# Four moves in an eight-stage layer stack: batch 0's preparation among feed-forward steps, keys beside the search for places, later results behind a lead, split maxima with priority

## The chip, the cores and the metric

The kernel runs on one core of a Trainium2 chip. A core has five engines with instruction queues of their own, each worked off in order: TensorE (PE in the profile; its weight loads are PEld), VectorE (DVE), ScalarE (ACT), GpSimd (POOL) and SyncE (SP), which here issues most DMA transfers. Engines wait for each other through semaphores. The metric is the device time of one execution in microseconds (us). Before the change the median of 3 runs is 3196.8 us (3187.31 to 3198.38).

## The reference

The input `x` has 4 batches of 512 rows of 512 numbers; a context `ctx_1024` has 4 x 512 rows of 256. Four layers each add a mixing block and a feed-forward block to `x`, each on the layer norm of `x` and behind a gate:

```python
x = x + tanh(g_xattn[0]) * L0_xattn(_layernorm(x), ctx_1024, ...)   # stage 0
x = x + tanh(g_ffn[0])   * L0_ffn(_layernorm(x), ...)               # stage 1
x = x + tanh(g_xattn[1]) * L1_xattn(_layernorm(x), ctx_1024, ...)   # stage 2
x = x + tanh(g_ffn[1])   * L1_ffn(_layernorm(x), ...)               # stage 3
x = x + tanh(g_xattn[2]) * L2_xattn(ctx_1024, _layernorm(x), ...)   # stage 4
x = x + tanh(g_ffn[2])   * L2_ffn(_layernorm(x), ...)               # stage 5
x = x + tanh(g_xattn[3]) * L3_xattn(_layernorm(x), ctx_1024, ...)   # stage 6
x = x + tanh(g_ffn[3])   * L3_ffn(_layernorm(x), ...)               # stage 7
```

The blocks that the change touches compute this:

```python
# L0_xattn: 16 heads of 32; softmax(q k^T) v over 496 keys, and over 16 more, added
# L0_ffn: relu((x @ sign(up).T) * up_scale) @ sign(down).T * down_scale * output_scale
# L2_xattn: a state-space scan over the context, gated by the normed x as z
xc = causal_conv(in_proj_w @ ctx, conv_w, 4 taps); u = silu(xc + conv_b)
dt_lo, Bm, Cm = split(x_proj_w @ u, (16, 16, 16))
delta = softplus(dt_proj_w @ dt_lo + dt_proj_b); A = -exp(A_log)
state = state * exp(delta * A) + (delta * u) * Bm;  y_t = sum_n state * Cm
y = (y + D * u) * silu(z)
# L2_ffn: top 2 of 8 experts per row, weights normalised; expert: (silu(x Wg) * (x Wu)) Wd
# L3_xattn: 32 heads of 16, q from x, k and v from ctx, axial rope on q and k, softmax, Wout
```

The scan of L2_xattn and the keys and values of L3_xattn depend on the context alone, not on `x`.

## The kernel before

`tile_blocks_kernel` (L2056) opens pools for a group of stages, runs them and closes the pools, so that the next group's tiles take the same memory. A scheduler puts each engine's instructions in order from their recorded priority and estimated readiness; `tc.high_priority(offset=...)` shifts the priority of what is recorded inside it, and `tied=True` products keep their recorded order on PE.

Stage 0 (`s0`): for each batch and each group of four heads a turn of products makes logits `s_ps`, and DVE takes their negated maxima per row (`s_nmx`, L694). `parted` (L644) splits each maximum on GpSimd into three 16-bit parts by copies and subtractions, PE transposes these (`s_ptm`), and they come off the logits `s_pl` before the exponential. `sums` (L751) takes the sums of the exponentials (`s_ri`, with a GpSimd multiply at L765).

Stage 1 (`s1`, L868): 4 batches x 2 halves x 8 double steps, 64 steps `f2`. A step makes `s_ph` (PE, L244), `s_hT` (ACT) and, one step behind, adds to four `s_acc` (PE, L905). Twice in a step `aside(1)` takes one yield from the generator `states()` (L1047), the state-space scan of stage 4, recorded at an offset of -4000. `states()` first loads its weights and yields; then it runs the nine pieces of batch 0 (`channels` 0 to 3, `low`, `raw`, `delta`, `raw`, `delta`) in one go and yields; both of these yields are taken ahead of the steps, by `next(states)` in the main function and in `s1`. Each of the 128 further yields makes two of 256 states: `s_db` on DVE, `s_da` on ACT, the scan `s_h` on DVE (L1158), its product with `s_C` on GpSimd (L1159), and sums over states on PE (`s_y`, L268). The next batch's pieces come between them. In a piece, `channels` has a product `s_pi`, its copy `s_xp` on ACT (L1095), and four taps on DVE (`s_xc`, the first at L1097, three more at L1099); `delta` has an add of 1 on DVE (L1129 is the step after it). `channels_done` ends a group of channels with two DVE steps on `s_ru` (L1195 and L1198). The signs of the feed-forward weights are ACT passes over `s1_wu` and `s1_wd` ahead of the steps.

Stages 2 to 4 run as generators, a batch apart, in 38 turns. Every second turn takes one piece of `keys()` (L1610), stage 6's keys and values: a product `s_pkv` on PE, `rope` on DVE (six steps, L1580 to L1582), the copy `s_vs` on ACT (L1673), DMA stores to `s_vd` and `s_kd`, and, for the piece before, eight transposes `pt_s6k` with an ACT scaling `s_kt` (L1690). There are 16 pieces and a last transposition, done by the end of stage 4.

Stage 5 (`s5`, L1510): `top2` routes rows to 8 experts (`s_pr`), `places` (L1313) finds where each row goes among 39 blocks of 128 rows of one expert each (a chain of small DVE steps with products `s_before`, `s_inside`, `s_inv` on PE), then `blocks` (L1454) runs the blocks: GpSimd gathers rows `s_xb`, PE transposes them and makes `pg_s`, DVE and ACT make `g_s`, PE makes `s_po`, GpSimd scatters the result to `s_ys`. A block's weights are four loads by SP into one of `ep` = 4 buffers (L1532 to L1537), each at the address of a register that SP reads from `ofi`.

Stage 6 (`s6`, L1693): `pieces(b)` prepares a batch. `results` (L1764) loads `s_y` (two buffers), adds stage 5's results to `x` (`residual`, L863: two DVE steps per tile of rows), loads the keys `s_kT` and values `s_v`, and makes the norm's statistics (`newton`, L186). Then come `xT`, `query` with `rope`, and `queryT`. A lead of 12 slots of maxima alone (`maxima`, DVE `s_top`, L1837) precedes the slots in which the products of weights and values run beside them. The pieces of batches 1 to 3 are dealt out over the slots of the batch before.

Of the kernel before, what the change touches and what calls it, by code (L numbers as in the profile page):

```python
# [48 lines left out]
class Net:  # L49
# [228 lines left out]
    def s0(self):  # L278
# [362 lines left out]
        def maxima():  # L641
# [26 lines left out]
            for b in range(NB):  # L668
                kT, qT = made[b][0:2]
                for g in range(4):  # L670
# [31 lines left out]
                    parted(b, g, nmx)  # L702
# [165 lines left out]
    def s1(self, states, aside):  # L868
# [26 lines left out]
        next(states)  # L895
# [23 lines left out]
        for i in range(2 * NB):  # L919
            b, cols = i // 2, slice(i % 2 * HT * P, (i % 2 + 1) * HT * P)  # L920
            for f2 in range(FC // 2):
                if i % 2 and f2 == 0 and b + 1 < NB:
                    xTs[b + 1] = self.lnT(f"s1_{b + 1}", b + 1)
                ph = self.mm(f"s1_ph_{i}_{f2}").rearrange("p (j n) -> p j n", j=2)
                for j in range(2):
                    fs = slice((2 * f2 + j) * P, (2 * f2 + j + 1) * P)
                    self.chain(
                        ph[:, j, :], [(wu[c][:, fs], xTs[b][:, c, cols]) for c in range(DC)],
                        tied=True,
                    )  # L930
                aside(1)
                behind.end()
                hT = self.t(f"s1_hT_{i}_{f2}").rearrange("p (j n) -> p j n", j=2)
                for j in range(2):
                    f = 2 * f2 + j
                    nc.scalar.activation(  # L936
                        hT[:, j, :], ph[:, j, :], AF.Relu, scale=us[:, f : f + 1]
                    )
                behind(down, i, f2, hT, more=True)
                aside(1)  # L940
# [106 lines left out]
    def states(self):  # L1047
# [31 lines left out]
        def pieces(b):  # L1079
# [3 lines left out]
            def channels(e):  # L1083
# [13 lines left out]
                nc.vector.tensor_scalar(xc, xp[:, 0:S], cw[:, e, 0:1], None, op0=ALU.mult)  # L1097
# [23 lines left out]
            def delta(es):  # L1121
# [5 lines left out]
                for z, z1 in zip(zs, z1s):  # L1127
                    nc.scalar.activation(z, z, AF.Exp, scale=-1.0)
                    nc.vector.tensor_scalar(z1, z, 1.0, None, op0=ALU.add)  # L1129
                    nc.vector.scalar_tensor_tensor(z, z1, -1.0, z, op0=ALU.add, op1=ALU.subtract)  # L1130
# [48 lines left out]
        yield  # L1179
# [7 lines left out]
        def channels_done(b, e, u, y):  # L1187
# [4 lines left out]
            nc.scalar.copy(r0, y[:, 0, :])  # L1192

            def rest():
                nc.vector.scalar_tensor_tensor(  # L1195
                    u, u, vec[:, 2, e : e + 1], r0, op0=ALU.mult, op1=ALU.add
                )
                nc.vector.tensor_tensor(u, u, r, op=ALU.add)  # L1198
                nc.sync.dma_start(rows[b]["y"][e * P : (e + 1) * P, :], u)
# [298 lines left out]
    def combine(self, name, weights, tiles, out=None):  # L1498

        ys = self.sorted[name][2][0 : 2 * NT * P, :].rearrange("(i t p) n -> t p i n", i=2, p=P)  # L1500
        for t in tiles:
            y = self.bp.tile([P, 2, D], F32, tag="y2", name=f"{name}_y2_{t}", bufs=self.y2)
            self.nc.sync.dma_start(y, ys[t])
            for i, w in enumerate(weights):
                self.residual(t, y[:, i, :], w[:, t : t + 1])
# [4 lines left out]
    def s5(self):  # L1510
# [11 lines left out]
        places, ofi = self.places("s5", hots, E)  # L1522

# [169 lines left out]
    def s6(self):  # L1693
# [12 lines left out]
        made, stats = {}, {}  # L1706
# [24 lines left out]
        def pieces(b):  # L1731
# [32 lines left out]
            def results():  # L1764

                self.combine("s5", self.wt5, range(b * TB, (b + 1) * TB))
# [24 lines left out]
        def maxima():  # L1791
# [18 lines left out]
            for b in range(NB):  # L1810
                kT, qT = made[b][0:2]
                for g in range(8):
                    for t in range(TB):
                        for y in range(2):
# [19 lines left out]
                            def after(ps=ps, dst=top[g % 2][:, t, 2 * y : 2 * y + 2, 16:17]):  # L1834
                                for i in range(2):
# [4 lines left out]
                                    ps[i][1](ins)  # L1840

# [214 lines left out]
def kernel(ctx: ExitStack, tc: tile.TileContext, a: dict, out: bass.AP):  # L2056
# [18 lines left out]
    with net.pools(cp=2, kp=1, rp=1, wp=8, bp=2, tp=14, sp=2, ps2=2, ps1=4):  # L2075
# [6 lines left out]


        stages = [net.s2(), net.s3(), net.s4()]
        turns = 0
        for step in range(NB + len(stages) - 1):
            going = [f(step - i) for i, f in enumerate(stages) if 0 <= step - i < NB]
            while going:
                going = [g for g in going if next(g, going) is None]
                turns += 1  # L2090
                if turns % 2:
                    aside(1)
        for _ in keys:
            pass
    net.y2 = 2
    with net.pools(op=1, ep=4, bp=1, up=3, tp=8, sp=2, ps2=2, ps1=4):
        net.s5()
# [88 lines left out]
```

## Time and profile before

| what | us |
|---|---|
| median of 3 runs | 3196.8 |
| the profiled execution, its own time | 3203.01 |
| its span | 3201.1 |
| stage 0, start to last `s_po` | 0 to 647 |
| first and last scan of the states | 695.5 and 1427.4 |
| stages 2 to 4, from the first `s_pq` to the end of stage 4's last transposes on PE | 1448 to 1738.5 |
| routing products `s_pr`, end | 1780.4 |
| first `pg_s` of stage 5 | 1815.4 |
| a block of stage 5 | 8.335 |
| stage 6, first `s_pq` | 2170.4 |

The mean granted clock of TensorE is 0.931 of full speed. The numbers behind an engine in a row of the profile are its busy time and, behind an x, its instructions. In an answer on waits a line has the waiting engine and what it wanted to do, then the engine and operation that released it, then the total in us, how often, and the longest. Rows of groups have line, engine, operation, output and input, shape and count, then busy us and mean ns of one, then the idle time of the engine just before them and who ended it.

### The profile page before, as it was taken

The numbers are of one execution on the slowest core, as the hardware profiler recorded it, in microseconds if no ns is written. First come the engines' busy times: TensorE is split into PE (matmuls) and PEld (weight loads), VectorE is DVE, ScalarE is ACT, GpSimd is POOL, SyncE is SP. The second block draws the span as 40 slices with busy tenths as digits, with TensorE's granted clock in tenths as the row PEclk, the third lists the DMA queues.
The fourth block names the chain that finished last, engine by engine and source line by source line (L and its number), as shares of the span: only waits on it lengthen the run. The fifth ranks groups of instructions, "written<-read, shape, count | busy, mean of one in ns | idle before, by whom it ended". The sixth has DMA issues, their size and how long they took to land.

```text
span 3201.1 us, 43082 instructions
## 1 busy us (share of the span) xinstructions
PE 2821.5 (88%) x15776; PEld 1442.0 (45%) x15776; DVE 1952.0 (61%) x3212; ACT 1196.0 (37%) x2061; POOL 975.8 (30%) x939
## 2 busy tenths in 40 slices
PE   6899898768988989997786699977999999989999
PEld 2333333234444444443344588862333333345774
DVE  6565666378897979987788311118666666735004
ACT  2343443365554445433222111112554545521331
POOL 3465654516555655760000122210000000001440
PEclk8899999879999989999897699997999999989999
DMA  4000000177676767862212599973000000013996
GB/s 133 7 1 7 1 1 1 20 252 238 195 229 176 236 206 224 250 196 84 77 64 90 176 320 326 322 259 137 14 29 14 29 1 1 1 53 122 379 384 225
DMA packets 266897, 438.75 MB, mean 137 GB/s; under 512 B 32400, under 2 KB 114576, under 8 KB 265152
## 3 DMA queue, kind: packets, MB, share of 16 engines
q1 hardware_dynamic: 250624, 386.72, 37.8%
q0 software_dynamic: 13760, 45.10, 3.9%
q10 hardware_dynamic: 2304, 4.20, 0.3%
q8 instruction: 126, 2.06, 0.3%
q14 instruction: 83, 0.68, 0.1%
HBM read 370.79 MB, written 65.13 MB: 136 GB/s over the span
## 4 chain that ended last, share of the span: by engine, by line
PE 60%; DVE 16%; POOL 9%; ACT 6%; issue 6%; DMA 3%; SPq 0%; DVEq 0%; POOLq 0%; ACTq 0%
PE s_pl L268 12%; PE s_po L244 11%; PE pg_s L244 7%; PE s_ph L244 6%; POOL s_h L1159 6%; PE s_pq L244 4%; PE s_av L268 3%; ACT pr_s L1957 2%; PE s_pb L244 2%; DVE s_h L1158 2%; PE s_acc L905 2%; PE s_pkv L244 1%; PE pt_s L223 1%; DVE x L863 1%; POOL es_s L746 1%
## 5 line engine op out<-in xcount | busy, mean ns | idle before, releaser
L1159 POOL TENSOR_TENSOR s_h<-s_h,s_C 128x512 f32<-128x512 f32 x256 | 448.1, 1751 | 290.3 <-DVE s_h L1158 248.6
L268 PE MATMUL s_pl<-s_qT,s_kT 32*128 32x512 f32 (+1 forms) x1536 | 447.3, 658 | 60.4 <-ACT pr_s L846 23.5
L268 PE MATMUL s_ps<-s_kT,s_qT 32*128 32x512 f32 (+1 forms) x1536 | 441.1, 677 | 12.7 <-DVE s_top L1837 5.9
L1837 DVE TENSOR_REDUCE s_top<-s_ps 128x1 f32<-128x512 f32 x512 | 328.5, 685 | 108.7 <-PE s_ps L268 108.6
L1957 ACT ACTIVATE pr_s<-s_pl 128x512 f32<-128x512 f32 x512 | 277.9, 595 | 307.4 <-PE s_ps L268 297.7
L1158 DVE TENSOR_TENSOR_SCAN s_h<-s_da,s_db 128x512 f32<-128x512 f32 x256 | 312.1, 1219 | 62.5 <-PE s_y L268 36.1
L1157 ACT ACTIVATE s_da<-s_rdl,s_A 128x512 f32<-128x512 f32 x256 | 184.4, 722 | 329.2 <-DVE s_h L1158 328.4
L1331 POOL MEMSET s_room<- 128x128 f32 (+1 forms) x2 | 0.5, 258 | 998.9 <-PE s_av L268 678.8
L268 PE MATMUL s_av<-pr_s,s_v 128*32 128x256 f32 (+1 forms) x3072 | 250.9, 398 | 0.2
L244 PE MATMUL s_ph<-xT_s,s_wu 128*128 128x256 f32 x1024 | 247.9, 397 | 0.7 <-ACT xT_s L161 0.7
L905 PE MATMUL s_acc<-s_wd,s_hT 128*128 128x512 f32 x512 | 239.9, 612 | 5.7 <-ACT s_hT L936 5.7
L244 PEld LDWEIGHTS s_ph<-xT_s,s_wu 128*128 128x128 f32 x1024 | 198.2, 198 | 78.8 <-issue 50.2
L244 PEld LDWEIGHTS pg_s<-s_xbT,s_w 128*128 128x128 f32 (+1 forms) x1872 | 214.7, 184 | 19.8 <-issue 17.8
L268 PEld LDWEIGHTS s_pl<-s_qT,s_kT 32*128 32x128 f32 (+1 forms) x1536 | 118.4, 186 | 227.1 <-ACT pr_s L1957 95.8
L244 PE MATMUL pg_s<-s_xbT,s_w 128*128 128x128 f32 (+1 forms) x1872 | 216.2, 276 | 1.4 <-ACT s_xbT L161 1.4
L694 DVE TENSOR_REDUCE s_nmx<-s_ps 128x1 f32<-128x496 f32 x256 | 158.4, 662 | 91.6 <-PE s_ps L268 81.3
L1156 DVE TENSOR_TENSOR s_db<-s_B,s_rdu 128x512 f32<-128x512 f32 x256 | 203.8, 796 | 10.7 <-DMA s_B<-s_bc 2.8
L846 ACT ACTIVATE pr_s<-s_pl 128x512 f32<-128x512 f32 (+1 forms) x256 | 138.7, 593 | 158.9 <-PE s_pl L268 82.9
L268 PE MATMUL s_y<-s_h,ident 64*64 64x512 f32 x1024 | 147.6, 640 | 49.5 <-issue 32.3
L268 PEld LDWEIGHTS s_av<-pr_s,s_v 128*32 128x32 f32 (+1 forms) x3072 | 61.4, 109 | 286.0 <-issue 253.9
L1552 DVE TENSOR_TENSOR g_s<-g_s,pg_s 128x256 f32<-128x256 f32 x78 | 27.5, 352 | 264.5 <-ACT g_s L1551 264.5
L1446 POOL DMA_INDIRECT s_xb<-s_xs,s_from x86 | 83.2, 968 | 333.0 <-PE ptr_s_xb L234 176.1
(388 smaller groups left out, 4460.4 us busy)
## 6 DMA issues: line engine op xcount, KB each, us to landing
s_B<-s_bc SPq DMA_DIRECT2D x256, 256.0 KB
s_C<-s_bc SPq DMA_DIRECT2D x256, 256.0 KB
s_w<-in_s_wg SPq DMA_DIRECT2D x39, 704.0 KB
s_w<-in_s_wu SPq DMA_DIRECT2D x39, 704.0 KB
s_w_rt<-in_s_ru SPq DMA_DIRECT2D x47, 512.0 KB
s_w_rt<-in_s_rd SPq DMA_DIRECT2D x47, 512.0 KB
s_w<-in_s_wd SPq DMA_DIRECT2D x39, 512.0 KB
s_y<-s_ys SPq DMA_DIRECT2D x32, 512.0 KB
```

Of the source, the lines that this page charges most:

```text
L244: ins = self.nc.tensor.matmul(out, lhsT=l, rhs=r, start=(i == 0), stop=(i == len(pairs) - 1)).ins
L268: ins = self.nc.tensor.matmul(out, lhsT=l, rhs=r, **flags).ins
L694: ins = nc.vector.tensor_reduce(nmx[:, at + i : at + i + 1], ps[i][0][:, 0:M], axis=AX.X, op=ALU.max, negate=True,).ins
L846: ins = nc.scalar.activation(prs[i][0:n, j, :], pl[j][0][0:n, :], AF.Exp).ins
L905: ins = nc.tensor.matmul(accs[i][t], lhsT=hT[:, j, t * P : (t + 1) * P], rhs=wd[f // 4][:, f % 4, :], start=(f == 0), stop=(f == FC - 1),).ins
L1156: nc.vector.tensor_tensor(db, br, du, op=ALU.mult)
L1157: nc.scalar.activation(da, dl, AF.Exp, scale=am[:, e, n : n + 1])
L1158: nc.vector.tensor_tensor_scan(h, da, db, 0.0, op0=ALU.mult, op1=ALU.add)
L1159: nc.gpsimd.tensor_tensor(h, h, cr, op=ALU.mult)
L1446: self.nc.gpsimd.indirect_dma_start(out=t, out_offset=None, in_=self.sorted[name][1], in_offset=bass.IndirectOffsetOnAxis(ap=fr[:, j : j + ...
L1837: ins = nc.vector.tensor_reduce(dst[:, i], ps[i][0], axis=AX.X, op=ALU.max, negate=True).ins
L1957: ins = nc.scalar.activation(prs[i][:, j, :], pl[j][0], AF.Exp).ins
```

## The change

The edits, by stage:

- `parted` in stage 0 is recorded at high priority.
- `next(states)` in `s1` goes. `states()` yields after each of batch 0's nine pieces and then three times more, so that these run in the first calls of `aside`; the first call in a step takes two yields where the step's number is 2 modulo 5, which makes 141 calls of 128.
- In the pieces the first tap of `s_xc` and the add of 1 go from DVE to ACT. In `channels_done` the two parts of the sum are added on GpSimd, and DVE has one step of two left.
- Stages 2 to 4 take a piece of `keys()` in every fourth turn. The rest is taken in stage 5 by one call behind `places`. The pools of `keys()` stay open through stage 5, and stage 5 has three buffers of weights (`ep`) where it had four.
- In stage 6 `lead` collects the instructions of the maxima. `combine` gets the last one recorded for batches 1 to 3, and orders its residuals behind it on DVE without a semaphore.

```diff
--- before.py
+++ after.py
@@ -699,7 +699,8 @@
 
                             yield parts, olds, after
                     waiting = b, g
-                    parted(b, g, nmx)
+                    with self.tc.high_priority():
+                        parted(b, g, nmx)
             turn(*waiting)
 
         queue, now = {}, [0]
@@ -892,7 +893,6 @@
 
         behind = Behind()
         xTs = {0: self.lnT("s1_0", 0)}
-        next(states)
         accs = {}
         HT = TB // 2
 
@@ -928,7 +928,8 @@
                         ph[:, j, :], [(wu[c][:, fs], xTs[b][:, c, cols]) for c in range(DC)],
                         tied=True,
                     )
-                aside(1)
+
+                aside(2 if (i * FC // 2 + f2) % 5 == 2 else 1)
                 behind.end()
                 hT = self.t(f"s1_hT_{i}_{f2}").rearrange("p (j n) -> p j n", j=2)
                 for j in range(2):
@@ -1094,7 +1095,7 @@
                 nc.gpsimd.memset(xp[:, 0:3], 0.0)
                 nc.scalar.copy(xp[:, 3 : S + 3], pi)
                 xc = self.t(f"s4_xc_{b}_{e}")
-                nc.vector.tensor_scalar(xc, xp[:, 0:S], cw[:, e, 0:1], None, op0=ALU.mult)
+                nc.scalar.mul(xc, xp[:, 0:S], cw[:, e, 0:1])
                 for k in range(1, 4):
                     nc.vector.scalar_tensor_tensor(
                         xc, xp[:, k : S + k], cw[:, e, k : k + 1], xc, op0=ALU.mult, op1=ALU.add
@@ -1126,7 +1127,7 @@
                 z1s = [self.t(f"s4_z1_{b}_{e}") for e in es]
                 for z, z1 in zip(zs, z1s):
                     nc.scalar.activation(z, z, AF.Exp, scale=-1.0)
-                    nc.vector.tensor_scalar(z1, z, 1.0, None, op0=ALU.add)
+                    nc.scalar.add(z1, z, 1.0)
                     nc.vector.scalar_tensor_tensor(z, z1, -1.0, z, op0=ALU.add, op1=ALU.subtract)
                 for z1 in z1s:
                     nc.scalar.activation(z1, z1, AF.Ln)
@@ -1176,7 +1177,11 @@
         yield
         for piece in pieces(0):
             piece()
-        yield
+            yield
+
+        for _ in range(3):
+            yield
+
         def row(k, b, e):
             t = self.qp.tile(
                 [P, S], F32, tag=f"r{k}", name=f"s4_r{k}_{b}_{e}", bufs=1 + (k != "u")
@@ -1190,12 +1195,12 @@
             nc.scalar.copy(r[0:64], y[64:128, 1, :])
             nc.scalar.copy(r[64:128], y[0:64, 1, :])
             nc.scalar.copy(r0, y[:, 0, :])
+            nc.gpsimd.tensor_tensor(r, r, r0, op=ALU.add)
 
             def rest():
                 nc.vector.scalar_tensor_tensor(
-                    u, u, vec[:, 2, e : e + 1], r0, op0=ALU.mult, op1=ALU.add
-                )
-                nc.vector.tensor_tensor(u, u, r, op=ALU.add)
+                    u, u, vec[:, 2, e : e + 1], r, op0=ALU.mult, op1=ALU.add
+                )
                 nc.sync.dma_start(rows[b]["y"][e * P : (e + 1) * P, :], u)
 
             return rest
@@ -1495,19 +1500,27 @@
 
         return self.nc.sync.value_load(ofi[0:1, j : j + 1], min_val=0, max_val=E - 1)
 
-    def combine(self, name, weights, tiles, out=None):
+    def combine(self, name, weights, tiles, out=None, after=None):
 
         ys = self.sorted[name][2][0 : 2 * NT * P, :].rearrange("(i t p) n -> t p i n", i=2, p=P)
         for t in tiles:
             y = self.bp.tile([P, 2, D], F32, tag="y2", name=f"{name}_y2_{t}", bufs=self.y2)
             self.nc.sync.dma_start(y, ys[t])
             for i, w in enumerate(weights):
-                self.residual(t, y[:, i, :], w[:, t : t + 1])
+                ins = self.residual(t, y[:, i, :], w[:, t : t + 1]).ins
+                if after is not None:
+                    self.tc.add_manual_dep(
+                        ins, after.name,
+                        mybir.DependencyInfo(
+                            mybir.DependencyClass.NoSync, mybir.DependencyReason.DATA
+                        ),
+                        reason="order on VectorE",
+                    )
             if out is not None:
                 self.nc.scalar.dma_start(out[t * P : (t + 1) * P, :], self.x[t])
 
 
-    def s5(self):
+    def s5(self, aside):
         nc, a = self.nc, self.a
         E, I = 8, 352
         parts = [(0, P), (P, P), (2 * P, I - 2 * P)]
@@ -1520,6 +1533,7 @@
             nc.vector.tensor_tensor(top, top, m, op=ALU.mult)
         wt = self.gated("s5", hots, tops, m, self.gf[:, 2:3])
         places, ofi = self.places("s5", hots, E)
+        aside()
 
         def up(j, xT):
             one = bass.ds(self.expert(ofi, j, E), 1)
@@ -1703,7 +1717,7 @@
             self.kq.tile([P, 4, S], F32, tag=k, name=f"s6_{k}_{b}_{y}") for y in range(2)
         ]
         LEAD = 12
-        made, stats = {}, {}
+        made, stats, lead = {}, {}, []
 
 
         banks = {"sc": 4, "pl": 3}
@@ -1763,7 +1777,8 @@
 
             def results():
 
-                self.combine("s5", self.wt5, range(b * TB, (b + 1) * TB))
+                tiles = range(b * TB, (b + 1) * TB)
+                self.combine("s5", self.wt5, tiles, after=lead[-1] if b else None)
                 for y in range(2):
                     nc.sync.dma_start(kT[y], self.k6[b][:, 4 * y : 4 * y + 4, :])
                 nc.sync.dma_start(va, self.v6[b].rearrange("(k p) n -> p k n", p=P))
@@ -1838,6 +1853,7 @@
                                             dst[:, i], ps[i][0], axis=AX.X, op=ALU.max, negate=True
                                         ).ins
                                     ps[i][1](ins)
+                                    lead.append(ins)
 
                             yield parts, olds, after
                     waiting = b, g
@@ -2072,7 +2088,9 @@
         net.s1(states, aside)
         for _ in states:
             pass
-    with net.pools(cp=2, kp=1, rp=1, wp=8, bp=2, tp=14, sp=2, ps2=2, ps1=4):
+    net.y2 = 2
+
+    with net.pools(cp=2, kp=1, rp=1):
         keys = net.keys()
 
         def aside(n):
@@ -2080,21 +2098,19 @@
                 for _ in range(n):
                     next(keys, None)
 
-
-        stages = [net.s2(), net.s3(), net.s4()]
-        turns = 0
-        for step in range(NB + len(stages) - 1):
-            going = [f(step - i) for i, f in enumerate(stages) if 0 <= step - i < NB]
-            while going:
-                going = [g for g in going if next(g, going) is None]
-                turns += 1
-                if turns % 2:
-                    aside(1)
-        for _ in keys:
-            pass
-    net.y2 = 2
-    with net.pools(op=1, ep=4, bp=1, up=3, tp=8, sp=2, ps2=2, ps1=4):
-        net.s5()
+        with net.pools(wp=8, bp=2, tp=14, sp=2, ps2=2, ps1=4):
+
+            stages = [net.s2(), net.s3(), net.s4()]
+            turns = 0
+            for step in range(NB + len(stages) - 1):
+                going = [f(step - i) for i, f in enumerate(stages) if 0 <= step - i < NB]
+                while going:
+                    going = [g for g in going if next(g, going) is None]
+                    turns += 1
+                    if turns % 4 == 1:
+                        aside(1)
+        with net.pools(op=1, ep=3, bp=1, up=3, tp=8, sp=2, ps2=2, ps1=4):
+            net.s5(lambda: aside(17))
     with net.pools(wp=2, kq=4, vp=2, up=1, rp=1, tp=8, bp=1, sp=2, ps3=4, ps1=1):
         net.s6()
     net.y2 = 7
```

## The prediction

> **What bounds the kernel now.** I read the page's busy shares first, then the span cut at the stage borders, then for each stretch the waits of the engine that is busiest in it, and the groups of stage 1.
>
> ```profile
> PE 2821.5 (88%) x15776; PEld 1442.0 (45%) x15776; DVE 1952.0 (61%) x3212; ACT 1196.0 (37%) x2061; POOL 975.8 (30%) x939
> ```
>
> PE at 88% looks like the bound, but the share is a mean over unlike stages. Cut by stage (columns: PE, PEld, DVE, ACT, POOL busy us, granted clock, DMA share, GB/s):
>
> ```profile
> 640.00:695.00 55.00, 36.01 (x80) 14.79 (x78) 34.67 (x66) 41.34 (x49) 0.78 (x5) 0.78 0.75 270
> 695.00:1100.00 405.00, 360.13 (x1398) 180.36 (x1399) 354.59 (x395) 202.83 (x308) 237.72 (x143) 0.92 0.72 216
> 1100.00:1440.00 340.00, 315.99 (x1287) 159.38 (x1289) 293.51 (x312) 151.51 (x241) 212.07 (x128) 0.96 0.73 218
> 1475.00:1743.00 268.00, 200.14 (x704) 105.65 (x704) 212.11 (x479) 75.14 (x107) 0.00 (x0) 0.88 0.23 74
> 1743.00:1780.00 37.00, 35.15 (x176) 33.82 (x176) 16.96 (x42) 6.21 (x12) 0.32 (x2) 0.55 0.25 96
> 1780.00:1815.00 35.00, 6.18 (x42) 5.02 (x42) 20.12 (x60) 0.52 (x2) 4.96 (x5) 0.50 0.66 219
> 1815.00:2143.00 328.00, 326.90 (x2258) 270.75 (x2258) 40.63 (x97) 56.87 (x137) 70.31 (x72) 0.99 0.90 302
> 2195.00:2240.00 45.00, 31.33 (x172) 9.06 (x176) 39.41 (x100) 9.48 (x18) 0.00 (x0) 0.62 0.16 47
> 2260.00:2420.00 160.00, 153.64 (x1240) 54.77 (x1232) 108.55 (x191) 83.26 (x155) 0.00 (x0) 1.00 0.06 21
> ```
>
> In stage 1 (first scan 695.5, last 1427.4) neither PE (676.1 of 745 us) nor DVE (648.1) is full: they take turns at being late. Stages 2 to 4 have PE at 75% and DVE at 79%, a chain through both. The search for places (1780 to 1815) has PE almost idle at half clock. The 39 expert blocks are PE's alone (326.9 of 328). The head of stage 6 (2195 to 2240) is DVE's, the rest PE's. DVE's waits in stage 1, then PE's:
>
> ```profile
> DVE s_h L1158 <- PE s_y L268: 36.1, 16, 6.3
> DVE s_r L916 <- PE s_acc L905: 10.3, 1, 10.3
> DVE s_xc L1097 <- ACT s_xp L1095: 5.3, 9, 0.6
> ```
>
> ```profile
> PE s_y L268 <- issue: 32.3, 11, 6.8
> PE s_y L268 <- POOL s_h L1159: 17.2, 6, 6.4
> ```
>
> **The sum** is made against the profiled execution, 3203.0 us; the median shown, 3196.8, is 6.2 below it.
>
> **A, split maxima with priority (stage 0).** It adds and removes nothing. In the built order PE, ACT, DVE and SP stand as before; on POOL the `s_ri` multiply (1.26 us) goes behind the second copy of the split in 4 of 15 turns, but stays ahead of the second subtraction, for which PE's transposes wait. Those four turns have PE idle of 1.89 us three times and 7.56 once. I take 0; ends 0 (nothing is released sooner) and -5 (a third of the 13.2 us of idle).
>
> **B, batch 0's preparation among the first steps.** Before, pieces 0 run from 646 to 695 with PE 36 of 55 us busy, and `s_ph` starts at 686.3. After, PE has 7 `s_ph` groups (3.65 us each) and 5 `s_acc` (3.63) ahead of the first `s_y`: 43.7 us of its 676 is done before the scans ask for it. The price: all four sign passes of `s1_wu` and one of `s1_wd` (1.9 us each) now precede batch 0's `s_xp` on ACT, so the first scan comes later. Five by 1.9, and one or two `s_ph` groups between pieces, are 13 to 17 us; I take +16. Then 256 states go at 141 calls in 64 steps in place of 128: per call PE has 7.28/2.2 + 1.09 = 4.4 us where it had 4.73, against 2 x 2.09 = 4.18 of DVE. The 36.1 us of DVE waiting on `s_y` should about halve (-18). Ends: none of it goes (0), or all (-36).
>
> **C, work off DVE in stage 1.** Rows of DVE, then what it moves:
>
> ```profile
> L1158 DVE TENSOR_TENSOR_SCAN s_h<-s_da,s_db 128x512 f32<-128x512 f32 x256 | 312.1, 1219 | 62.5 <-PE s_y L268 36.1 <-ACT s_da L1157 0.5 <-ACT s_hT L936 0.4
> L1198 DVE TENSOR_TENSOR s_ru<-s_ru,s_yr 128x512 f32<-128x512 f32 x15 | 10.2, 681 | 0.2
> L1097 DVE TENSOR_SCALAR s_xc<-s_xp,s_cw 128x512 f32<-128x512 f32 x12 | 8.7, 727 | 5.3 <-ACT s_xp L1095 5.3
> ```
>
> L1097 leaves with 8.7 us busy, but the first `scalar_tensor_tensor` then waits for one more ACT instruction (about 0.6 after the 0.6 of the copy) and the 5.3 us of waiting stay or grow to 10: net -4. The 12 `s_z1` adds beside states take 5 us at 0.42. L1198 leaves with 10.2; POOL takes 16 adds at 1.27 to 1.77 (20 to 28 us; POOL is busy 449.8 of 745), each in the queue of the products `s_h` for which `s_y` already waited 17.2 us. ACT gets 24 instructions of about 0.6 (busy 354 of 745). I take -18; ends -26 and +5 (POOL's adds hold `s_y` as often as now).
> B and C: +16 - 18 - 18 = -20 if the waits halve; beside that, the last batch of states took 153 us at 32 calls of 4.73, PE's pace, and would go at 4.4: -10. Together -30, ends -53 and +10.
>
> **D, results of batches 1 to 3 behind the lead.** Before, these three (8 residuals of 0.745, 4 statistics of 0.68 and 15 tiny ones, 12 us each) sit between 2168 and 2233 on DVE. The lead's maxima ended 3 to 4 us late, and nine slots from 2210.8 to 2238 took 27.2 us where later ones take 1.8 each: 16.2. Some 15 us are lost. After, batch 1's 12 us come among slots 3 to 8, batches 2 and 3 later. A slot of 1.8 has 1.36 of maxima, so DVE catches up slowly: half the loss returns. I take -7; ends -15 and +2. SP now loads both `s6_kT` of batch 0 ahead of the first `s_y`, and `s6_wq` and `s6_wo` already among the blocks; PE's 23.6 us wait at 2143 loses about 1. Later `s_kT` loads stand behind `s_y` loads that wait for residuals, with a batch (160 us) to spare: 0.
>
> **E, keys beside the search.** Six and a half pieces (PE 3.6 + 1.0, DVE 6 x 0.41, ACT 0.6 + 1.0) leave stages 2 to 4. If all were in the way there, PE would give back 30 us and DVE 16; if all lie in gaps, 0. With PE 25% and DVE 21% idle I take -10 (ends 0 and -30).
> They arrive in stage 5. What PE waited for in 1743 to 1816:
>
> ```profile
> PE s_inv L1418 <- DVE s_what L1411: 13.6, 2, 9.4
> PE ptr_s_xb L234 <- DMA s_xb<-s_xs,s_from: 9.0, 1, 9.0
> PE s_before L1328 <- DVE s_room L1325: 6.0, 1, 6.0
> ```
>
> In PE's built order one piece's products and eight transposes stand inside the routing, which has no gap. Ahead of `s_before` come eight transposes, one product group and four transposes: 5.2 us at full clock, about 10 at half, for a gap of 6.0. Ahead of the first `s_inv` two groups and 12 transposes (8.8 or 17) for 9.4; ahead of the second 3.7 or 7 for 4.2. At full clock the gaps hold them, at half clock they are late by 4 + 8 + 3. DVE's rope steps (2.5 us a piece, 15 in all) stand inside the chain of small operations too, and its 20.1 of 35 leaves them 15. I take +8 in the routing and +6 in the search, +14; ends -5 and +35. SP's key stores stand ahead of the index load and the first weights, each waiting for ACT's `s_vs`: inside this range.
> The clock decides a part of this. From 1741.8 to 1775.9 PE is 95% busy and yet gets half the clock. The Trainium skill (TensorE: Matmul & The Clock Gate, "What's actually happening") gives full clock after about 3.4 us of sustained work; this row disagrees, since its small products keep PE occupied for 34 us and get none. By the page the keys would run cold only at first and E in stage 5 would be about +4; by the row, half clock, about +20.
>
> **Three weight buffers for four (`ep`).** A buffer is held from its block's `pg_s` to its last `s_po`, 16.4 us. At 8.335 us a block, four leave 33.3 - 16.4 = 16.9 us from issue to need, three leave 8.6. In the trace's packets the gate and up weights issued at 1833.0 were in at about 1836.5 and 1838.6, 3.5 and 5.6 us after issue. PE stays the cover: 0; ends 0 and +54 (1.5 us late in each of 36 blocks).
>
> Sum: 0 - 30 - 7 - 1 - 10 + 14 + 0 = -34: 3203 - 34 = 3169 in the profile, less 6 is **3163** against the median.
>
> **The rivals.** (1) Three buffers make the blocks wait for weights. For it: SP waited 186.6 us for `s_po` before issuing, and DMA is at 0.90; against: 5 us of slack at 3 buffers. It decides once a block slips 0.95 us (36 x 0.95 = 34); at 1.5 it is +54: 3217. (2) Stage 1 gives nothing: DVE's waits on `s_y` become waits on POOL, and the first scan's +16 eats the rest. B and C 0: 3193. (3) Keys at half clock and in DVE's chain: +35 in stage 5 in place of +14, the rest as forecast: 3184. (4) Everything at its better half: B and C -50, E -20 with +5, D -12: 3203 - 78 - 6 = 3119.
>
> **How the numbers follow.** Forecast 0.46, (1) 0.10, (2) 0.16, (3) 0.12, (4) 0.10, and 0.06 for several worse ends at once, above 3215. A measurement here tells 0.5%, 16 us, from no change: faster is under 3181, slower over 3213. The forecast's own range is 3140 to 3182. Faster: 0.44 of the forecast, (4), a third of (3) and of (2): 0.64. Same: most of the rest, 0.20. Slower: (1) and the worse ends, 0.16. The range, 3125 to 3215, leaves out most of (4) and the worse half of slower.
>
> **What would show it.** Right: first scan near 711, last near 1395 to 1402; DVE's waits on `s_y` under 20; stages 2 to 4 about 10 shorter; `pg_s` of block 0 over 38 us after the last `s_pr` (35.0 before); blocks still 8.335 apart; slots even at 1.8 sooner in stage 6. Wrong: PE waiting for `s_w` among the blocks, `s_y` waiting for POOL more than 30 us, stage 5's head over 100 us where it was 72.

## The result, and the profile after

The change makes the kernel slower: 3225.6 us (median of 4 runs, 3221.0 to 3227.7) against 3197.0 before, a ratio of 1.0089 (95% interval 1.0072 to 1.0107). The forecast was 3163 with a range of 3125 to 3215; both sign and size were wrong.

The profiled execution after took 3223.93 us with a span of 3222.2, so the two profiles differ by 21.1 in span, of the 28.6 between the medians: the profile before, 3203.0, was a long one of its kernel. The other 7.5 us have no place in these two profiles. Cut at the same instructions in both traces, the 21.1 us lie here (the last column is the prediction's own sum for that stretch):

| stretch | before | after | difference | forecast |
|---|---|---|---|---|
| stage 0, to its last `s_po` | 646.8 | 650.3 | +3.6 | 0 |
| to the first scan of the states | 48.7 | 61.7 | +13.0 | +16 |
| first scan to last `s_acc` (stage 1) | 744.3 | 737.1 | -7.1 | -46 |
| stages 2 to 4, to the first `s_pr` | 303.5 | 298.1 | -5.5 | -10 |
| routing, to the last `s_pr` | 37.1 | 35.4 | -1.6 | +8 |
| search, to the first `pg_s` | 35.0 | 42.7 | +7.6 | +6 |
| 39 blocks, to the last `pg_s` | 323.0 | 327.9 | +4.9 | 0 |
| to the first `s_pq` of stage 6 | 32.2 | 32.4 | +0.2 | -1 |
| to the 40th maximum `s_top` | 68.7 | 61.0 | -7.7 | -7 with the next row |
| to the last maximum | 564.4 | 578.3 | +13.9 | |
| the rest, stage 7 in it | 397.5 | 397.2 | -0.3 | 0 |

Windows of the changed kernel, in the columns of the windows before (us, then busy time of PE, PEld, DVE, ACT and POOL, granted clock, DMA share, GB/s):

```profile
712.00:1100.00 388.00, 340.26 (x1340) 169.24 (x1339) 333.48 (x371) 204.92 (x314) 241.11 (x148) 0.93 0.71 218
1100.00:1440.00 340.00, 305.08 (x1229) 152.62 (x1231) 278.92 (x299) 156.62 (x249) 224.44 (x136) 0.92 0.75 221
1747.00:1783.00 36.00, 35.63 (x197) 31.65 (x195) 12.14 (x30) 8.80 (x13) 0.32 (x2) 0.67 0.23 81
1783.00:1825.00 42.00, 27.56 (x120) 16.15 (x120) 28.70 (x91) 8.35 (x12) 5.91 (x6) 0.83 0.75 255
```

In stage 1 DVE's busy share fell, yet PE's did not rise: both engines stand still more. In the routing and the search the clock rose from 0.55 and 0.50 to 0.67 and 0.83; how much of the routing's -1.6 this is worth is taken up below (E3). DVE's waits between first scan and last `s_acc`, changed kernel (waiting engine and what it wanted, what released it; us in total, times, longest):

```profile
DVE s_ru L1201 <- POOL s_yr L1198: 39.8, 13, 12.6
DVE s_h L1159 <- PE s_y L268: 24.5, 20, 5.7
DVE s_xc L1100 <- ACT s_xc L1098: 12.1, 9, 1.3
DVE s_z L1135 <- ACT s_z L1133: 5.3, 6, 1.2
```

The first line is new, and larger than the 36.1 us on `s_y` that the change was to halve. But 12.6 us of it are one wait behind the last scan, where before DVE stood 10.3 us for `s_acc`; 27.2 us in 12 places lie among the scans. PE's waits in the same stretch, the third of these before the change, then PE's waits in the first blocks, and around the middle batches of stage 6:

```profile
PE s_y L268 <- POOL s_h L1160: 27.8, 7, 5.6
PE pt_s L223 <- DVE xl_s L205: 21.7, 3, 11.0
PE s_y L268 <- issue: 19.6, 5, 5.7
```

```profile
PE pt_s L223 <- DVE xl_s L205: 13.9, 3, 4.6
```

```profile
PE pg_s L244 <- DMA s_w<-in_s_wg: 3.2, 2, 1.7
```

```profile
PE s_pl L268 <- DVE s_top L1852: 6.3, 4, 1.8
```

The last two did not exist before: PE waits for weights among the blocks, and for DVE's maxima in stage 6. `xl_s` are the next batch's normalised rows, which PE transposes.

What PE waits for ahead of an `s_y` is not what these lines name. One place of the changed kernel:

```profile
1294.41 0.72 ACT L1158 ACTIVATE s_da<-s_rdl,s_A 128x512 f32<-128x512 f32 x1 [1.36 <-DVE s_h L1159]
1295.16 0.58 ACT L1195 COPY s_yr<-s_y 64x512 f32<-64x512 f32 x1
1296.35 0.58 ACT L1197 COPY s_y<-s_y 128x512 f32<-128x512 f32 x1
1297.04 1.98 PE L268 MATMUL s_y<-s_h,ident 64*64 64x512 f32 x8 [5.59 <-POOL s_h L1160]
```

The pool of `s_y` has one buffer (`psb=1`). After each group of 16 states ACT copies the sums out in three copies, and PE's first sum of the next group, which writes the same buffer, follows 0.1 us behind the last copy. From the second group on, all of PE's idle places over 1 us ahead of an `s_y` lie at such a change of group and end so: 11 places with 39.7 us before, 13 with 51.4 us in the changed kernel, and likewise in every other run. GpSimd, which the profile names, had made five to seven of the new group's products by then. In one place of the changed kernel the profile names the copy itself (4.1 us). Here ACT's copies stand in its queue behind `s_da`, which waited for DVE's scan.

### The profile page after: what moved, and what is told of

Its sections match the earlier page's. It is cut to its first block, busy times and chain, and to the rows that moved or that the text cites. A ratio compares the mean times of both kernels' runs of the same rounds, so it can differ in the third digit from the quotient of the medians.

```text
span 3222.2 us, 42968 instructions
## 1 busy us (share of the span) xinstructions
PE 2835.0 (88%) x15776; PEld 1445.7 (45%) x15776; DVE 1909.6 (59%) x3164; ACT 1220.0 (38%) x2097; POOL 994.0 (31%) x955
## 4 chain that ended last, share of the span: by engine, by line
PE 33%; issue 9%; DVE 8%; POOL 4%; ACT 3%; DMA 2%; SPq 1%; POOLq 0%; DVEq 0%; ACTq 0%
PE s_pl L268 8%; PE s_po L244 6%; PE s_ph L244 5%; ACT pr_s L1973 2%; PE s_pb L244 2%; PE s_pq L244 2%; PE s_av L268 2%; POOL s_h L1160 2%; DVE x L864 1%; PE s_acc L905 1%; POOL s_ys L1478 1%; PE s_pr L244 1%; PE s_pkv L244 1%; DVE st_s L174 1%; POOL s_xb L1451 1%
## 5 line engine op out<-in xcount | busy, mean ns | idle before, releaser
L268 PE MATMUL s_pl<-s_qT,s_kT 32*128 32x512 f32 (+1 forms) x1536 | 451.0, 663 | 68.7 <-ACT pr_s L847 23.7
L1159 DVE TENSOR_TENSOR_SCAN s_h<-s_da,s_db 128x512 f32<-128x512 f32 x256 | 312.1, 1219 | 53.8 <-PE s_y L268 24.5
L847 ACT ACTIVATE pr_s<-s_pl 128x512 f32<-128x512 f32 (+1 forms) x256 | 138.7, 593 | 160.4 <-PE s_pl L268 88.4
L1157 DVE TENSOR_TENSOR s_db<-s_B,s_rdu 128x512 f32<-128x512 f32 x256 | 190.8, 745 | 9.9 <-DMA s_B<-s_bc 1.7
L268 PE MATMUL s_y<-s_h,ident 64*64 64x512 f32 x1024 | 148.3, 653 | 51.4 <-POOL s_h L1160 27.8
```

Source lines behind the costliest of these rows:

```text
L268: ins = self.nc.tensor.matmul(out, lhsT=l, rhs=r, **flags).ins
L847: ins = nc.scalar.activation(prs[i][0:n, j, :], pl[j][0][0:n, :], AF.Exp).ins
L1157: nc.vector.tensor_tensor(db, br, du, op=ALU.mult)
L1159: nc.vector.tensor_tensor_scan(h, da, db, 0.0, op0=ALU.mult, op1=ALU.add)
```

## The experiments

Times of single runs of one kernel spread by up to 19 us, so the times carry the ratio to the kernel before, and the stretches of the table, read from each run's trace, carry the causes. Where the code of a stretch is the same, most of them repeat well: end of stage 0 to the first scan 61.7 in each of eight traces with the pieces in the fixed calls of the change, the routing 35.4 in nine. Stage 0 itself, with one and the same code, ended anywhere from 641.5 to 650.9, stages 2 to 4 took 293.7 to 298.1, and the search 42.7 to 45.3. From the end of stage 0 to the last `s_acc` six traces with the change's stage 1 took 798.1 to 802.1, and two with the stage 1 of before 790.1 and 793.0, so that a difference of up to 4 us there shows no effect. The runs that take one part back (E1, E2, E3 and E7) lie 8 to 12 us below the changed kernel's median, while their stretches are only 3 to 9 us shorter; where the rest lies was not found. "E1" to "E11" number the runs.

**E1, the add of `channels_done` back on DVE.**

```diff
-            nc.gpsimd.tensor_tensor(r, r, r0, op=ALU.add)
...
-                    u, u, vec[:, 2, e : e + 1], r, op0=ALU.mult, op1=ALU.add
+                    u, u, vec[:, 2, e : e + 1], r0, op0=ALU.mult, op1=ALU.add
                 )
+                nc.vector.tensor_tensor(u, u, r, op=ALU.add)
```

> The changed kernel with the sum of the two parts in channels_done back on DVE (two steps on s_ru, none on GpSimd); all else as changed. Theory 1, the GpSimd add stands behind the products s_h in its queue and DVE stands still for it (39.8 us in 13 places in the changed trace): these waits go, 16 steps of 0.68 (11 us) come back to DVE, and a part returns as waits on s_y; 20 to 29 us faster than the changed kernel, 3197 to 3206, the last scan near 1410. Theory 2, stage 1 is paced by PE and GpSimd and DVE only waits elsewhere: within 8 us of the changed kernel, 3218 to 3226, and DVE's waits on s_y grow by 25 to 30 us.

Measured: 3217.7, ratio 1.0072 (1.0046 to 1.0099). First scan to last `s_acc` 733.8, 3.3 less than with the add on GpSimd. DVE's waits in this run:

```profile
DVE s_h L1159 <- PE s_y L268: 34.1, 28, 6.4
DVE s_ru L1200 <- ACT s_y L1197: 13.0, 3, 11.1
DVE s_xc L1100 <- ACT s_xc L1098: 12.1, 9, 1.3
DVE s_z L1135 <- ACT s_z L1133: 6.0, 6, 1.3
```

Theory 2 is nearer, though the waits on `s_y` grew by 10 us and not by 25 to 30. The 39.8 us of waiting for GpSimd are gone, and as much stands in their place: 19 us of work (the two steps take 31.0, the one that was left took 12.0), 13 us of waiting for ACT's copies, 11.1 of them behind the last scan, and 10 us more on `s_y`. So the new wait, though it is the largest line, was worth 3 us of stage 1; 733.8 lies below the 736.4 to 740.4 of the six traces with the add on GpSimd.

**E2, the residuals free of the lead.**

```diff
-                self.combine("s5", self.wt5, tiles, after=lead[-1] if b else None)
+                self.combine("s5", self.wt5, tiles, after=None)
```

> The changed kernel with the residuals of batches 1 to 3 free of the lead again (after=None); all else as changed. Theory 1, the order moved the results of batches 2 and 3 into the full slots, where they cost 7.8 and 6.2 us (seen near slots 160 and 286 of the changed trace), and gave 7.7 us in the first batch: taking it away gains 6 us, 3217 to 3221, with the lead later by 8 and no steps of 7.8 and 6.2 later. Theory 2, the steps near slots 160 and 286 come from the later loads of s_y alone: they stay, the lead gets 8 later, 3230 to 3234.

Measured: 3213.9, ratio 1.0046 (1.0029 to 1.0063). The stretch to the 40th maximum is 66.3 (61.0 with the order), the rest to the last maximum 564.4 (578.3). Theory 1: the order gives 5 to 8 us at the head and loses 13.9 later, a net loss of 6 to 9.

**E3, the keys as before, four buffers.** The loop over stages 2 to 4 with a piece in every second turn, pools and `ep=4` as in the kernel before.

```diff
-        with net.pools(op=1, ep=3, bp=1, up=3, tp=8, sp=2, ps2=2, ps1=4):
-            net.s5(lambda: aside(17))
...
+    with net.pools(op=1, ep=4, bp=1, up=3, tp=8, sp=2, ps2=2, ps1=4):
+        net.s5(lambda: None)
```

> The changed kernel with the keys in every second turn of stages 2 to 4 as before, none in stage 5, and four weight buffers; all else as changed. Theory 1, the move gave 5.2 us in stages 2 to 4 and cost 7.6 ahead of the blocks and 4.9 among blocks 2 to 6 (the loads of s6_wq and s6_wo ahead of weights): 7 us faster than the changed kernel, 3217 to 3220, all blocks 8.335 apart. Theory 2, the slip among the blocks is the ramp of the weights whatever the buffers, and the search's lengthening is paid back by the shorter stages: within 3 us of the changed kernel.

Measured: 3215.6, ratio 1.0064 (1.0038 to 1.0089). Stages 2 to 4 take 304.7 (298.1), the routing 34.9 (35.4), the search 34.8 (42.7), the blocks 322.8 (327.9). Theory 1: the keys' move is 6.6 us of gain against 0.5, 7.9 and 5.1 of loss, 7 us slower in sum. The routing without any keys is 34.9 here and in E11, and 37.1 in E10 and before: the -1.6 of the table is no gain from the keys.

**E4, batch 0's preparation ahead of the steps** (with E1's edit, so to be compared with E1).

```diff
         xTs = {0: self.lnT("s1_0", 0)}
+        next(states)
...
-                aside(2 if (i * FC // 2 + f2) % 5 == 2 else 1)
+                aside(1)
...
             piece()
-            yield
-
-        for _ in range(3):
-            yield
-
+        yield
```

> The kernel of the run before the last two (the add back on DVE) with batch 0's preparation ahead of the steps again, as before the change (next(states) in s1, one yield for all nine pieces, one yield in each call). It is to be compared with that run, not with the changed kernel. Theory 1, the preparation among the steps is worth its later first scan: this is 5 to 15 us slower than with it. Theory 2, the later first scan (16.6 us, the first s_y 24.9 us) is not won back, because DVE has its work to do whenever it begins: this is 5 to 15 us faster.

Measured: 3215.9, ratio 1.0056 (1.0038 to 1.0075); E1 has 3217.7. From the end of stage 0 to the last `s_acc` this run takes 792.9 and E1 795.5. The difference, 2.6 us in favour of the early preparation, is below either theory's 5 and within what one code varies by, and the times say "same": no worth of the preparation among the steps is seen. The run also shows the two moves to ACT by themselves, since only they distinguish its stage 1 from that before: 792.9 against 793.0. Among DVE's waits between the scans:

```profile
DVE s_h L1160 <- PE s_y L268: 34.7, 19, 6.4
DVE s_xc L1101 <- ACT s_xc L1099: 12.1, 9, 1.3
DVE s_z L1136 <- ACT s_z L1134: 2.7, 5, 1.0
```

DVE was relieved of 14 us (677.6 busy before, 663.7 here, both from the end of stage 0 to the last `s_acc`); 9.5 of it came back between the scans as waits for ACT, whose queue now holds the first tap (12.1 where it was 5.3 for the copy) and the add (2.7). Ahead of the scans the moves cost more: the first scan comes 52.5 us after stage 0 where it came 48.7, and the 3.9 us gained behind it pay that back.

**E5, residuals behind the first lead only.**

```diff
-                self.combine("s5", self.wt5, tiles, after=lead[-1] if b else None)
+                self.combine("s5", self.wt5, tiles, after=lead[2 * LEAD - 1] if b else None)
```

> The changed kernel with the residuals of batches 1 to 3 all ordered behind the last of the 24 maxima of the first lead (lead[2 * LEAD - 1]), in place of the last maximum recorded. They then stand on DVE between slots 16 and 50 of batch 0, none in batches 1 and 2. Theory 1, a result (12 us of DVE) costs what it has beyond the slots' own gaps wherever it stands in one lump: the losses near slots 160 and 286 (7.8 and 6.2) go and two like them come in batch 0: within 4 us of the changed kernel, 3222 to 3228. Theory 2, it costs so much in later batches because products of weights and values are at full pace there, and little in batch 0, where PE still fills: 8 to 14 us faster, 3212 to 3218.

Measured: 3224.4, ratio 1.0093 (1.007 to 1.0116). To the 40th maximum 71.0, from there to the last 570.0: 641.0 in all, where the changed kernel has 639.3, E2 630.7 and the kernel before 633.1. Theory 1: no place in the full slots is cheap. The losses in batches 1 and 2 are gone, and as much has come in batch 0.

**E6, the results of batches 2 and 3 in four pieces each.**

```diff
...
-            out = [results] + 3 * [lambda: None] + [lambda: xT(0), lambda: xT(1)]
+            out = [results] + 3 * [lambda: None]
+            if b > 1:
+                out = [lambda t=t: results(t) for t in range(TB)]
+            out = out + [lambda: xT(0), lambda: xT(1)]
```

> The changed kernel with the results of batches 2 and 3 dealt out as four pieces, one tile of rows with its statistics each (two residuals, 2.2 us with the statistics), in the places of the one piece and the three empty ones behind it. Theory 1, the loss in the later batches is a matter of the lump: a slot of 1.8 us has 0.5 us of DVE to spare, four or five slots hold one tile, and the steps near slots 160 and 286 shrink from 14 us in all to under 4: 10 to 14 us faster than the changed kernel, 3212 to 3216. Theory 2, the loss comes from the loads of s_y that stand ahead of the keys, or from the statistics' last steps: the steps stay above 10.

Measured: 3214.2, ratio 1.0075 (1.0049 to 1.0101). From the 40th to the last maximum 574.0, between the 578.3 of one lump and the 564.4 without: measured against the kernel before, the slots fall back by 4.5 and 5.1 us in place of 7.7 and 6.2. The time lies in theory 1's range, but the steps are in neither's: dealing out gives back 4.3 of 13.9. What holds the other 9.6 us was not separated.

**E7, the loads of `s6_wq` and `s6_wo` behind the last block's weights.**

```diff
+        lq = nc.sync.dma_start(wq, a["s6_wq"].rearrange("(c p) n -> p c n", p=P))
+        self.tc.add_manual_dep(
+            lq.ins, self.lastw.ins.name,
+            mybir.DependencyInfo(mybir.DependencyClass.NoSync, mybir.DependencyReason.DATA),
...
+        lo = nc.sync.dma_start(wo, a["s6_wo"].rearrange("(c p) n -> p c n", p=P))
...
```

> The changed kernel with SP's loads of s6_wq and s6_wo ordered behind the last load of a block's weights. Theory 1, blocks 2 to 6 slipped 4.9 us because these two loads of 1 MB stand in SP's queue ahead of weights that have only 8.6 us: all blocks 8.335 apart, about 5 us faster, 3219 to 3222, and stage 6 begins no later after the last block. Theory 2, three buffers are too few at the start whatever else is loaded: the slip stays above 3 us.

Measured: 3215.0, ratio 1.0072 (1.0043 to 1.0101); the blocks take 323.0, as with four buffers, and PE's wait for weights is gone. Theory 1. The queue of SP in the changed kernel shows why (start us, us, engine, line, operation, output and input):

```profile
1845.04 0.41 SPq L1712 DMA_DIRECT2D s_wq<-in_s_wq  x1
1845.71 0.40 SPq L1546 DMA_DIRECT2D s_w<-in_s_wg  x1
...
1856.80 0.45 SPq L1933 DMA_DIRECT2D s_wo<-in_s_wo  x1
1862.39 0.37 SPq L1546 DMA_DIRECT2D s_w<-in_s_wg  x1
```

A load of 1 MB stands ahead of the weights of block 3, and one ahead of those of block 5. Blocks 3 to 6 start 1.6, 2.3, 4.2 and 4.6 us later against block 2 than before, and all later ones keep the 4.6. Before the change both loads were issued at 2133 us, behind the last block's weights. Whether it is their place in the queue or their share of the transfers that holds the weights up was not separated.

**E8, eight buffers of `s_h`** (with E1's edit).

```diff
-                for k, bufs in (("B", 4), ("C", 5), ("da", 2), ("h", 7))
+                for k, bufs in (("B", 4), ("C", 5), ("da", 2), ("h", 8))
```

> The run with the add back on DVE (the first of the earlier runs), and eight buffers of s_h where it has seven. To be compared with that run. Theory 1, DVE cannot run ahead of PE for want of buffers, so that what PE saves in the plain steps comes back as waits of about 4 us at the 13 doubled calls: one more state lets DVE run 2.1 us further ahead, up to 13 times 2.1 = 27 us; 8 to 25 us less between the first scan and the last s_acc (733.8 in that run). Theory 2, DVE's own work and its waits on ACT and DMA set the pace, the waits of PE are only what is left: less than 3 us.

Measured: 3217.3, ratio 1.0061 (1.0043 to 1.0079); first scan to last `s_acc` 730.3 against E1's 733.8. The 3.5 us are at the edge of theory 2 and far from the 8 to 25 of theory 1; the same stretch with the same code differed by 3.1 between E10 and the kernel before. The six traces of the change's stage 1 lie 4.0 apart in this stretch. Room for states is not what holds stage 1.

**E9, the calls dealt evenly** (with E1's edit): 141 calls over 256 quarters of steps.

```diff
+        def tick():
+            units[0] += 1
+            total = 4 * NB * FC
+            aside(units[0] * 141 // total - (units[0] - 1) * 141 // total)
...
-                aside(2 if (i * FC // 2 + f2) % 5 == 2 else 1)
+                    tick()
...
-                aside(1)
```

> The run with the add back on DVE, and the 141 calls of stage 1 dealt evenly over quarters of the steps (two halves of s_ph, two halves of s_acc, 256 quarters), in place of two or three at fixed places of a step. To be compared with that run. Theory 1, what PE saved by its early groups came back at the 13 doubled calls, where two sums stand without PE work between them and PE waits (50.5 us there): evenly dealt, the pace is 4.4 us a call, PE's waits on s_y fall under 25 us, and first scan to last s_acc falls from 733.8 to 710 to 725. Theory 2, the order of calls does not matter, DVE's lumps of channel work do: within 4 us of 733.8, PE's waits stay above 40.

Measured: 3210.8, ratio 1.005 (1.0029 to 1.0072). First scan to last `s_acc` 719.1, inside theory 1's range; but the first scan comes 8.7 us later still (70.4 after stage 0), since the first calls are rarer, so that the whole from stage 0 to the last `s_acc` falls only from 795.5 to 789.5. PE's idle time over 1 us ahead of an `s_y`, from the trace, is 37.5 us in 9 places (50.4 in 13 in E1), not under theory 1's 25; meanwhile PE's waits for `s_hT` rose from 4.3 to 19.7 us, and all of its idle time in the whole stretch only fell from 88.4 to 86.3. Nor do the doubled calls make E1's 13 places: in its trace ten pairs of sums have no product between them, and two of the 13 places, 7.9 us, lie at one. All 13, and the 9 here, lie at the changes of group described above. So the rhythm cost 6 us at most.

**E10, the priority of the split alone, on the kernel before.**

```diff
-                    parted(b, g, nmx)
+                    with self.tc.high_priority():
+                        parted(b, g, nmx)
```

> The kernel before with the split of the maxima at high priority alone. Theory 1: no change, within 5 us of the kernel before; stage 0 ends between 641 and 651, as it did in profiles of one and the same code. Theory 2, the changed kernel's stage 0, 3.6 us longer in its profile, is this edit's: 3 to 5 us slower.

Measured: 3197.8 over 10 runs, ratio 1.0009 (0.9995 to 1.0022). Theory 1; stage 0 ended at 645.5.

**E11, the preparation among the steps and even calls alone, on the kernel before** (with `tick` as in E9).

```diff
-        next(states)
...
-                aside(1)
...
+                    tick()
...
             piece()
-        yield
+            yield
+
+        for _ in range(3):
+            yield
```

> The kernel before with batch 0's preparation among the steps and the calls dealt evenly over quarters, nothing else of the change. Theory 1, as for the even calls above, PE's early 43.7 us stay saved: end of stage 0 to last s_acc falls from 793.0 by 10 to 20, 3177 to 3187. Theory 2, it is neutral as the fixed calls were: 3192 to 3200.

Measured: 3192.1 over 12 runs, ratio 0.9998 (0.9985 to 1.0011): no change. Its trace has 789.1 from stage 0 to the last `s_acc` where the kernel before has 793.0. E10's trace, with the stage 1 of before, has 790.1, so nothing is left of the gain. The preparation, even with calls that are dealt better than in the change, beats the changed kernel and not the one before.

## Why the prediction was wrong, point by point

**A** was right: 0 forecast, E10 no change. The 3.6 us of stage 0 between the two profiles are no cause: stage 0 of the same code varied by 9.4.

**B**, "per call PE has 7.28/2.2 + 1.09 = 4.4 us where it had 4.73 [...] should about halve (-18)", and the -10 for the last batch, failed. The later first scan was right (+13.0 for +16), and DVE's waits on `s_y` did fall, from 36.1 to 24.5; but other waits took their place. The average of 4.4 is no pace: it counts PE's work alone and leaves out where PE stands still. The work done early was overrated too: one of the seven `s_ph` groups stood ahead of the first `s_y` before. PE was busy for 64.8 us ahead of its first sum in place of 29.2, but that sum came 21.3 us later (73.0 us after stage 0 for 51.7). The 14.3 us that this leaves were more than lost again behind it: PE's waits at the changes of group, short ones too, rose from 41.3 to 51.4 us, and those for the next batch's rows from 13.9 to 21.7. The last batch took 155.9 us, not 143. E4 prices the whole of B at +2.6, below what the times or the traces resolve. Evenly dealt it is 6.0 us better (E9) or, on the kernel before, 1.0 to 3.9 (E11), no measurable gain.

**C**, "I take -18", failed on both halves. The first tap and the add of 1 were taken at -4 and -5 and are worth -0.1 (E4), that is nothing: the wait for ACT took their place. The add on GpSimd was taken for a load on GpSimd's queue that holds up `s_y`; what waited instead was DVE itself, whose last step needs the sum, 39.8 us in 13 places, 27.2 of them among the scans. DVE was relieved of even more than the 10.2 us forecast, 19 us, since the step that was left got shorter as well. Undoing it gave 3.3 us. The larger mistake stands behind both: I treated DVE's busy time as what stage 1 pays for. From the end of stage 0 to the last `s_acc` the whole took 789 to 802 us in all variants, while DVE's work there fell from 677.6 to 637.1; PE's stayed:

```profile
647.00:1440.00 793.00, 705.12 (x2748) 351.49 (x2750) 677.63 (x759) 393.51 (x593) 450.38 (x274) 0.93 0.73 219
```

```profile
650.00:1449.00 799.00, 708.15 (x2753) 354.60 (x2752) 637.09 (x711) 410.75 (x626) 467.58 (x288) 0.92 0.71 216
```

(the kernel before, then the changed one). PE has 705 of 793 us of its own, so the room was under 90 us, and none of the changes took any of it: PE's idle time there is 84 to 94 us in all 13 traces. Of the 88 before, 41.3 lie at the changes of group, where PE waits for ACT to copy `s_y` out of its one buffer, 19.5 ahead of the first scan, 13.9 at the next batch's rows and 5.7 at `s_hT`. No forecast term looked at the buffer of `s_y`. No run gave it a second one, so what that would be worth stays open; more buffers of `s_h` (E8) and an even rhythm (E9) did not settle it.

**D** was half right. The 7.7 us gained to the 40th maximum match the forecast's -7, partly by luck: 15 were to be gained and half to return, and the trace has 10.5 at the 32nd maximum, of which 2.8 are lost again by the 40th, where batch 1's results stand. "A slot of 1.8 has 1.36 of maxima, so DVE catches up slowly: half the loss returns" leaves no more than that for all three batches, and batches 2 and 3 cost another 7.7 and 6.2 us: there the products of weights and values are at full pace and PE waits for the maxima. The true term is +6, not -7 (E2). E5 shows that the head of stage 6, where PE still waits for loads and the first products, is nearly the cheapest place for them; the early position that I read as a defect was the better one.

**E** came out near its sum, +0.5 before the blocks for +4, with errors that cancel: stages 2 to 4 gave 5.5 for 10, and the routing took nothing where +8 stood. The search got 7.6 us longer by the mechanism named, products ahead of the counts on PE (start us, us, engine, line, operation, output and input, count, and the idle time before it):

```profile
1786.60 5.36 PE L244 MATMUL s_pkv<-s_wkv,ctx_s 128*128 128x512 f32 x8 [1.11 <-ACT s_kt L1704]
1791.79 0.60 PE L1618 MATMUL pt_s6k<-ident,s_k_r 128*128 128x128 f32 x4
1792.23 0.39 PE L1333 MATMUL s_before<-s_room,tri 128*128 128x128 f32 x2
...
1822.94 1.97 PE L1618 MATMUL pt_s6k<-ident,s_k_r 128*128 128x128 f32 x8 [1.17 <-ACT s_vs L1687]
1825.43 0.79 PE L244 MATMUL pg_s<-s_xbT,s_w 128*128 128x128 f32 x2 [0.53 <-ACT s_kt L1704]
```

`s_before` comes 9.5 us after the last `s_pr` where it came 5.9 after. The last transposes of the keys lie between the gathered rows (1820.65) and block 0, which begins 4.8 after these where it was 1.8. The routing, forecast 8 longer, took 35.4 us, 1.6 less than before and 0.5 more than in the two traces of E3 and E11 that have no keys in it either: the half clock that the forecast went by did not hold there with the keys (0.67).

**Three buffers.** "PE stays the cover: 0" was right for the weights themselves, and rival 1, that three buffers make the blocks wait, was wrong as put: from block 7 on the blocks are 8.335 us apart. But I had seen in the built order that "`s6_wq` and `s6_wo` already among the blocks" and counted it as a gain of 1 for stage 6; past which waiting load they were moved I did not ask. They cost 4.9 (E7).

The sum by these measured terms: B and C +5.9, D +6.2, E +0.5, blocks +4.9, stage 0 +3.6, in all 21.1 with the rounding and the small rest; stage 0's share is no effect of the change, which leaves 17.5. Rival 2, stage 1 gives nothing (B and C 0), came nearest; it was given 0.16 and ended at 3193, because every other part was left at its forecast beside it.

## What to carry to other kernels

An average pace per call says nothing where engines hand work to each other through a few buffers: list the places where the fullest engine stands still and see what ended each, also past the releaser that the profile names, and ask which engine's busy time is nearly the whole of the stretch before work is moved off another. Work that is ordered behind something must be followed to where it lands: a lump that costs little where engines wait for loads costs half of its length or more in a full pipeline (12 us of DVE work cost 7.7 and 6.2 here). A large load that is issued early ahead of others is a cost to those as soon as they have only a few us to spare.

## What the runs showed of the hardware

PE's granted clock did not follow its busy time. In the routing before, PE was busy 33.3 of 35.0 us (1741 to 1776) at a clock of 0.51; with one piece's eight products of 512 columns and eight transposes among the same small products the routing ran at 0.67, and the search rose from 0.50 to 0.83. The routing without them took 37.1 us at 0.55 in two traces (before and E10) and 34.9 us at 0.58 and 0.59 in two others (E11 and E3), since a group of 32 `s_pr` took 4.3 to 4.8 us or 6.8 to 7.0; with them it took 35.4. So the added work was nearly free there. Stage 0 of one and the same code ended between 641.5 and 650.9 us in the traces; why was not studied.
